# A four-layer graph network on one core: two waits moved back, epsilon off VectorE, and the last groups' evacuations on ScalarE

## The chip, the cores and the metric

One core of one Trainium2 chip. The metric is the device time of one execution in microseconds (us); the kernel before took 1694.29 us (median of three runs, 1689.37 to 1699.63). Engines are named as the profile names them: PE (TensorE, matmuls), DVE (VectorE), ACT (ScalarE), POOL (GpSimd), SP (SyncE, which here issues DMAs).

## The reference

128 graphs of 64 nodes with 128 features each, and one weighted adjacency `adj` per graph, about one entry in four not zero. Four layers, each `x = layernorm(x + layer(x, adj))`; the layernorm is `(x - m) / sqrt(v + 1e-5)` over the features, without a weight.

- Layers 0 and 1 are continuous-filter convolutions: for each edge its weight is expanded into 20 (64) gaussians, sent through a two-layer net with shifted softplus between, multiplied by the neighbour's features, summed over the neighbours, and sent through a two-layer node net.
- Layer 2 is a graph convolution: with `A = D^-1/2 (adj + I) D^-1/2`, `h = elu(elu(x W0 + b0))`, `h = elu(A (h W1) + b1)`, `out = A (h W2) + b2`.
- Layer 3 is `relu((A x) W^T + b)` with a nearly equal `A`.

## The kernel before, in words

The kernel uses that the graphs are sparse. Each row's entries that are not zero are packed into slots, and the filter net of layers 0 and 1 runs on the slots alone. The 128 graphs are sorted by their number of entries and taken in 64 pairs (128 partitions hold the 64 nodes of two graphs); eight pairs make a *set*, with a common slot size (`CAPS`), and four pairs make a *group*, which shares the node work. Flags are gathered for every assumption (row and graph fit their slots, the exponentials stay in range), and a dense program would run if one failed; it doesn't with these inputs.

**The loop.** `sparse_stack` writes out one long list of instructions by hand. Layer 0's 64 pairs and then layer 1's 64 pairs are taken in three chunks each, 384 turns in all. A turn issues `filter_in` for the newest chunk (matmul px, L1753, then two ACT steps), `filter_out` for the one two turns back (matmul pw, L1766), `message` (DVE, m, L1794), `gather` for the one between (matmul pg, L1779, and an ACT copy), and `slot_sums` (DVE, agg, L1818). Between these stand queues of generators, each advanced by a few steps per turn:

- `early`: `gathering()`, which packs set after set (`compact`), then looks at crowded rows, then runs `bounded()`, waits for the queue `side` to be empty, runs `settle()` (which makes the flag) and `late_constants()` (degrees). It gets 9 steps per turn at first, then 2, 5, 5, then 7. A bare `yield` is a step in which nothing is issued, and `wait_steps(n)` is n of them; `PACE` is 4.
- `side`: two steps per turn. `spread` scatters packed rows by an index (`goes`), loads them back in sorted order and packs them for layer 1. For sets 0 and 1 it is `spread_again` (L1228), which first scatters and reloads the adjacency rows in sorted order (`permuted(s, True)`, eight scatters on POOL, each with two loads on SP), then computes `goes` from them in `goes_on` (L1072, a DVE instruction at L1075).
- `befores`, `nodes`, `convs`, `last`: the node work of each group, one step per turn. A step that ends in `yield True` has issued a matmul into PSUM; what empties that PSUM is issued only after the next queue's step.
- `stores`: the scatters of finished rows to the output, one per turn, on POOL.

The order of the list is binding: `in_order` ties every engine's instructions to their place, so on each engine a waiting instruction holds up all that stands behind it.

**The parts that are touched.** `bounded()` (L1234) checks that the first filter net stays small: for each of the two layers it loads a weight and a bias on SP (L1241, L1243), four steps later takes absolute values on DVE (L1245, L1246), four steps later sums with a small matmul (L1249) and compares (L1250, L1251). `layernorm` (L1393) computes mean and variance (st, mv) on DVE, adds epsilon on DVE (rs, L1403), then takes the power -1/2: on POOL for a group of four pairs (L1406), with Ln and Exp on ACT for smaller groups; the normalised rows (L1411) are written by POOL for four pairs and by DVE otherwise. It is called 70 times, 61 of them for four pairs.

`graph_convs` (L1640) holds layers 2 and 3 of a group: transpose (gx), W0 (gh0), `elu` (L1590) with its negative part m and positive part r (L1594, L1595), exponentials on ACT, W1 (hw), `A` (gh1), elu, W2, `A` (o2), residual and layernorm, `A` again (sup), W3 (o3), residual and layernorm, and the store. Its results leave PSUM by DVE copies: gxt (L1664) and gy in `times` (L1653). For layer 1 the groups are numbered 0 to 17: 0 to 13 are four pairs each (sets 1 to 7), 14 is pairs 0 to 3, 15 is pairs 4 and 5, 16 and 17 are one pair each. The convolutions of groups 14 to 17 come after the last turn of the loop, in a loop that takes one step of each queue in rotation. Stores of groups 0 to 13 are indirect scatters from POOL; those of the last four are plain DMAs from SP (L1715).

Of the kernel before, what the change touches and what calls it, by code (L numbers as in the profile page):

```python
# [12 lines left out]
F32 = mybir.dt.float32  # L13
AF = mybir.ActivationFunctionType
ALU = mybir.AluOpType
# [4 lines left out]
P = 128  # L20
# [6 lines left out]
LN_EPS = 1e-5  # L27
# [574 lines left out]
def sparse_stack(ctx: ExitStack, tc: tile.TileContext, t: dict, out: bass.AP, flag):  # L602
# [11 lines left out]
    nc = tc.nc  # L614
    x, adj = t["x"], t["adj"]
    NB = x.shape[0]
    NP = NB // 2
    GS = 4
    PACE = 4


    GROUPS = [[slice(GS * q, GS * (q + 1)) for q in range(NP // GS)]]
# [3 lines left out]
    const = ctx.enter_context(tc.tile_pool(name="sconst", bufs=1))  # L626
# [41 lines left out]
    nc.vector.memset(half, 0.5)  # L668
    one = const.tile([P, 1], F32, name="one")
    nc.vector.memset(one, 1.0)  # L670
    neg_one = const.tile([P, 1], F32, name="neg_one")
    nc.vector.memset(neg_one, -1.0)

# [120 lines left out]
    def wait_steps(n):  # L794
        yield from (None for _ in range(n))
# [73 lines left out]
    with (  # L869
# [31 lines left out]
        to = const.tile([NB, 1], U32, name="graph_to")  # L901
# [36 lines left out]
    def act(out_, in_, func, **kw):  # L938
        nonlocal fence, latest, kind
        now = func == AF.Sin  # L940
        if kind is None or now != kind:
            fence = latest
            if not now:
                ctx_ = tc.issue_after(fence.ins) if fence is not None else nullcontext()
                with ctx_:
                    fence = nc.scalar.preload_act_table_set("natural_log_exp_and_others")
            kind = now
        with tc.issue_after(fence.ins) if fence is not None else nullcontext():
            latest = nc.scalar.activation(out_, in_, func, **kw)  # L949
        return latest  # L950
# [276 lines left out]

    def spread_again(s, comb):  # L1228
        yield from permuted(s, True)
        yield  # L1230
        goes_on(s)
        yield from spread(s, comb)

    def bounded():  # L1234


        for i, (w, b, k) in enumerate(
            (("L0_gnn_fw1", "L0_gnn_fb1", NG0), ("L1_gnn_W1T", "L1_gnn_b1", NG1))
        ):
            w1 = big(f"w1_{i}", C)[0:k]  # L1240
            nc.sync.dma_start(w1, t[w])  # L1241
            b1 = const.tile([P, 1], F32, name=f"b1_{i}")
            nc.sync.dma_start(b1, column(b))  # L1243
            yield from wait_steps(PACE)
            nc.vector.scalar_tensor_tensor(w1, w1, -1.0, w1, ALU.mult, ALU.max)  # L1245
            nc.vector.scalar_tensor_tensor(b1, b1, -1.0, b1, ALU.mult, ALU.max)  # L1246
            yield from wait_steps(PACE)
            u = ps_n.tile([P, 512], F32, tag="n", name=f"sum_{i}")
            nc.tensor.matmul(u[:, 0:1], lhsT=w1, rhs=one[0:k], start=True, stop=True)  # L1249
            nc.vector.tensor_add(b1, b1, u[:, 0:1])  # L1250
            nc.vector.tensor_scalar(odd[:, 1 + i : 2 + i], b1, X_LIMIT, None, ALU.is_gt)  # L1251
            yield from wait_steps(PACE)
# [140 lines left out]
    def layernorm(y, dst, n, name):  # L1393

        stats = node.tile([P, GS, 6], F32, tag="st", name=f"st_{name}")[:, 0:n]
        mv = node.tile([P, GS, 2], F32, tag="mv", name=f"mv_{name}")[:, 0:n]
        for s in range(n):
            nc.vector.bn_stats(stats[:, s, :], y[:, s, :])
            nc.vector.bn_aggr(mv[:, s, :], stats[:, s, :])
            if s + 1 == GS // 2 < n:  # L1400
                yield
        rstd = node.tile([P, GS], F32, tag="rs", name=f"rs_{name}")[:, 0:n]
        nc.vector.tensor_scalar(rstd, mv[:, :, 1], LN_EPS, None, ALU.add)  # L1403
        yield
        if n == GS:
            nc.gpsimd.tensor_tensor(rstd, rstd, neg_half[:, 0:n], ALU.pow)  # L1406
        else:
            act(rstd, rstd, AF.Ln)
            act(rstd, rstd, AF.Exp, scale=-0.5)
        for s in range(n):  # L1410
            (nc.gpsimd if n == GS else nc.vector).tensor_scalar(  # L1411
                dst[:, s, :], y[:, s, :], mv[:, s, 0:1], rstd[:, s : s + 1],
                ALU.subtract, ALU.mult,
            )
        yield
# [174 lines left out]
    def elu(ps, bias, i, q):  # L1590

        n = ps.shape[1] // P
        m, r = tiled(f"em{i}", n, q), tiled(f"er{i}", n, q)
        nc.vector.tensor_scalar(m, ps, bias, 0.0, ALU.add, ALU.min)  # L1594
        nc.vector.tensor_scalar(r, ps, bias, 0.0, ALU.add, ALU.max)  # L1595
        yield
        act(m, m, AF.Exp)
        if i == 0:
            act(m, m, AF.Exp, bias=neg_one)
        yield  # L1600
        nc.vector.scalar_tensor_tensor(r, m, 1.0, r, ALU.subtract, ALU.add)
        yield
        return by_pair(r)
# [12 lines left out]
    def normal(i, q, nT):  # L1616
# [7 lines left out]
        dinv = g[f"dinv{i}"][:, pairs]  # L1624
        nc.vector.tensor_mul(nT, ps, dinv.unsqueeze(2).to_broadcast([P, n, P]))

    normals = {}

    def normals_of(q):
# [10 lines left out]
    def graph_convs(q):  # L1640

        pairs = GROUPS[1][q]
        xs = x_all[:, pairs, :]
        n = xs.shape[1]

        def times(name, lhs, rhs):

            _, ps = bank(f"{name}_{q}", n)
            for s in range(n):
                nc.tensor.matmul(ps[:, s, :], lhsT=lhs(s), rhs=rhs(s), start=True, stop=True)  # L1650
            yield True
            y = by_pair(tiled(f"gy_{name}", n, q))
            nc.vector.tensor_copy(y, ps)  # L1653
            yield
            return y

        if n == GS:
            scaled(2, q)
        flat, ps = bank(f"gx_{q}", n)
        for s in range(n):  # L1660
            nc.tensor.transpose(ps[:, s, :], xs[:, s, :], ident)
        yield True
        xt = tiled("gxt", n, q)
        nc.vector.tensor_copy(xt, flat)  # L1664
        nc.gpsimd.tensor_tensor(xs, xs, g["b2"].unsqueeze(1).to_broadcast([P, n, C]), ALU.add)
        yield
        flat, _ = bank(f"gh0_{q}", n)
        nc.tensor.matmul(flat, lhsT=g["W0"], rhs=xt, start=True, stop=True)
        yield True
        h = yield from elu(flat, g["b0"], 0, q)  # L1670
        y = yield from times("hw1", lambda s: h[:, s, :], lambda s: g["W1"])
        if n == GS:
            nT = by_pair(tiled("nTs2", n, q))
            yield from normal(2, q, nT)
            yield
        else:
            nT = normals[2, q]
        flat, ps = bank(f"gh1_{q}", n)
        for s in range(n):
            nc.tensor.matmul(ps[:, s, :], lhsT=y[:, s, :], rhs=nT[:, s, :], start=True, stop=True)  # L1680
        yield True
        h1 = yield from elu(flat, g["b1"], 1, q)
        y2 = yield from times("hw2", lambda s: h1[:, s, :], lambda s: g["W2"])
        _, ps = bank(f"o2_{q}", n)
        for s in range(n):
            nc.tensor.matmul(ps[:, s, :], lhsT=nT[:, s, :], rhs=y2[:, s, :], start=True, stop=True)
        if n == GS:
            scaled(3, q)
        yield True
# [12 lines left out]
        nc.tensor.matmul(  # L1702
            flat, lhsT=ones, rhs=g["b3"][:, 0:n, :].rearrange("i s c -> i (s c)"),
            start=True, stop=False,
        )
        for s in range(n):
            nc.tensor.matmul(ps[:, s, :], lhsT=y3[:, s, :], rhs=g["W3"], start=False, stop=s == n - 1)
        yield True
        z = by_pair(tiled("gz3", n, q))
        nc.vector.scalar_tensor_tensor(z, ps, 0.0, xs, ALU.max, ALU.add)  # L1710
        yield
        yield from layernorm(z, z, n, f"3_{q}")
        if pairs.start < 8:
            b = 2 * pairs.start
            nc.sync.dma_start(out[b : b + 2 * n].rearrange("(s b) n c -> (b n) s c", b=2), z)  # L1715
        else:
            stores.append(store_rows(pairs, z))
# [111 lines left out]

    befores, nodes, convs, sums = deque(), deque(), (deque(), deque()), deque()  # L1830
    small_groups, small = range(NP // GS - 1, len(GROUPS[1])), {}
    last = {q: deque() for q in small_groups}
    stores = deque()
    slot_data, messages, aggs = {}, {}, {}
# [61 lines left out]
    for i in range(3 * N + 2):  # L1896
        n, k = divmod(i, 3)
# [113 lines left out]
```

## Time and profile before

| what | value |
|---|---|
| median of three runs | 1694.29 us |
| the profiled execution | 1692.3 us, its span 1690.4 us |
| PE busy | 1529.1 us, 90% of the span |
| DVE busy | 1509.3 us, 89%, 4125 instructions |
| ACT busy | 1351.8 us, 80% |
| POOL busy | 721.1 us, 43% |
| mean granted TensorE clock | 0.966 |
| epsilon adds (L1403) | 70, together 21.5 us of DVE |

The shares are means over stages with different limits: in the page's forty slices DVE is fullest up to about 700 us, PE from about 800 to 1550 us, and in the last two slices all engines fall off and the clock drops to 0.8 and 0.6. The chain that ended last is led by PE (32% of the span), with DVE 11%, POOL 7% and DMA 6%. A line such as `DVE m L1794 <- PE pw L1766` is read: DVE, about to write m at line 1794, waited for PE's pw of line 1766. A chain "piece" is time that could not have been shorter without that instruction being shorter or earlier.

### The profile page before, as it was taken

The numbers are of one execution on the slowest core, as the hardware profiler recorded it, in microseconds if no ns is written. First come the engines' busy times: TensorE is split into PE (matmuls) and PEld (weight loads), VectorE is DVE, ScalarE is ACT, GpSimd is POOL, SyncE is SP. The second block draws the span as 40 slices with busy tenths as digits, with TensorE's granted clock in tenths as the row PEclk, the third lists the DMA queues.
The fourth block names the chain that finished last, engine by engine and source line by source line (L and its number), as shares of the span: only waits on it lengthen the run. The fifth ranks groups of instructions, "written<-read, shape, count | busy, mean of one in ns | idle before, by whom it ended". The sixth has DMA issues, their size and how long they took to land.

```text
span 1690.4 us, 24016 instructions
## 1 busy us (share of the span) xinstructions
PE 1529.1 (90%) x6813; PEld 790.9 (47%) x6813; DVE 1509.3 (89%) x4125; ACT 1351.8 (80%) x1699; POOL 721.1 (43%) x1119
## 2 busy tenths in 40 slices
PE   1289999999889999998999999999999999998975
PEld 1134444444444444454444555555555555544444
DVE  7689999999979999789888999999999999988875
ACT  1369898989788989697999888898898888887831
POOL 2424455444645433133412354444554444554344
PEclk9999999999989999798999999999999999999986
DMA  7656554556454544344666465555465455465100
GB/s 253 197 127 144 126 139 119 130 125 157 117 123 120 142 114 116 90 130 106 150 149 133 116 144 128 119 134 134 114 141 126 114 133 125 115 143 131 45 6 21
DMA packets 119055, 211.22 MB, mean 125 GB/s; under 512 B 46830, under 2 KB 70656, under 8 KB 118272
## 3 DMA queue, kind: packets, MB, share of 16 engines
q1 hardware_dynamic: 107760, 193.11, 47.6%
q0 software_dynamic: 6576, 14.99, 2.8%
q10 hardware_dynamic: 4576, 1.49, 0.4%
q8 instruction: 56, 0.92, 0.2%
q14 instruction: 87, 0.71, 0.2%
HBM read 190.86 MB, written 18.64 MB: 124 GB/s over the span
## 4 chain that ended last, share of the span: by engine, by line
PE 32%; DVE 11%; issue 8%; POOL 7%; DMA 6%; ACT 4%; SPq 1%; DVEq 0%; POOLq 0%; ACTq 0%
PE pw L1766 11%; PE pg L1779 7%; PE px L1753 6%; DMA out_dram<-gz,at_row 5%; POOL x_all L1411 3%; DVE m L1794 3%; DVE agg L1818 2%; POOL rs L1406 1%; ACT h L949 1%; POOL gz L1411 1%; PE hw L1650 1%; DVE hot L1738 1%; ACT d L949 1%; ACT g L949 1%; PE back L1577 1%
## 5 line engine op out<-in xcount | busy, mean ns | idle before, releaser
L949 ACT ACTIVATE g<-pg 128x672 f32<-128x672 f32 (+12 forms) x384 | 298.8, 778 | 134.3 <-PE pg L1779 129.4
L949 ACT ACTIVATE h<-h,half 128x672 f32<-128x672 f32 (+13 forms) x385 | 351.1, 912 | 12.5
L1779 PE MATMUL pg<-hot,ys 64*128 64x336 f32 (+12 forms) x1536 | 352.6, 537 | 4.7 <-ACT g L949 4.6
L1818 DVE TENSOR_REDUCE agg<-m 128x16 f32<-128x240 f32 (+13 forms) x896 | 324.8, 410 | 2.4
L1766 PE MATMUL pw<-h,w_L_gnn_fw 128*128 128x336 f32 (+6 forms) x768 | 279.6, 489 | 38.9 <-DVE m L1794 38.8
L1766 PE MATMUL pw<-h,w_L_gnn_W2T 128*128 128x420 f32 (+5 forms) x768 | 303.1, 517 | 3.0 <-DVE m L1794 3.0
L1794 DVE SCALAR_TENSOR_TENSOR m<-pw,c_L_gnn_b,g 128x420 f32<-128x420 f32 (+5 forms) x384 | 226.0, 625 | 10.9 <-PE pw L1766 8.1
L1794 DVE SCALAR_TENSOR_TENSOR m<-pw,c_L_gnn_fb,g 128x336 f32<-128x336 f32 (+6 forms) x384 | 201.9, 564 | 25.9 <-PE pw L1766 19.6
L949 ACT ACTIVATE h<-px,c_L_gnn_b 128x840 f32<-128x840 f32 (+5 forms) x192 | 176.8, 921 | 44.6 <-PE px L1753 44.3
L1779 PEld LDWEIGHTS pg<-hot,ys 64*128 64x128 f32 x1536 | 118.6, 189 | 187.3 <-ACT h L949 98.9
L1766 PEld LDWEIGHTS pw<-h,w_L_gnn_fw 128*128 128x128 f32 x768 | 138.6, 199 | 135.8 <-DVE m L1794 84.7
L1753 PE MATMUL px<-d,fw 32*128 32x336 f32 (+6 forms) x768 | 170.8, 522 | 29.5 <-ACT d L949 28.6
L1766 PEld LDWEIGHTS pw<-h,w_L_gnn_W2T 128*128 128x128 f32 x768 | 133.1, 191 | 129.3 <-DVE m L1794 32.3
L1406 POOL TENSOR_TENSOR rs<-rs,neg_half 128x4 f32<-128x4 f32 x61 | 67.8, 1111 | 276.8 <-DVE rs L1403 275.4
L1738 DVE SCALAR_TENSOR_TENSOR hot<-j,row,w 128x1212 f32<-128x1212 bf16 (+12 forms) x128 | 175.7, 1373 | 8.8 <-DMA w<-w_dram 8.8
L949 ACT ACTIVATE h<-px,c_L_gnn_fb 128x672 f32<-128x672 f32 (+6 forms) x192 | 158.3, 824 | 20.8 <-PE px L1753 15.6
L1753 PE MATMUL px<-d,w1t 64*128 64x420 f32 (+5 forms) x768 | 169.8, 519 | 0.0
L949 ACT ACTIVATE d<-d,neg_off 128x1212 f32<-128x1212 f32 (+12 forms) x128 | 136.4, 1065 | 8.0 <-DMA d<-d_dram 8.0
L1028 POOL DMA_INDIRECT rows<-comb,goes x64 | 68.9, 1076 | 117.7 <-DMA rows<-comb,goes 75.9
L1753 PEld LDWEIGHTS px<-d,fw 32*128 32x128 f32 x768 | 60.3, 191 | 124.8 <-issue 46.9
L1411 POOL TENSOR_SCALAR x_all<-ny,mv,rs 128x128 f32<-128x128 f32 x124 | 108.5, 881 | 3.4
L1028 POOL DMA_INDIRECT out_dram<-gz,at_row x56 | 71.3, 1273 | 50.5 <-DMA out_dram<-gz,at_row 39.8
(261 smaller groups left out, 2206.6 us busy)
## 6 DMA issues: line engine op xcount, KB each, us to landing
d<-d_dram SPq DMA_DIRECT2D x32, 315.0 KB
w<-w_dram SPq DMA_DIRECT2D x32, 315.0 KB
d<-d_dram SPq DMA_DIRECT2D x32, 303.0 KB
w<-w_dram SPq DMA_DIRECT2D x32, 303.0 KB
w<-w_dram SPq DMA_DIRECT2D x32, 252.0 KB
j<-j_dram SPq DMA_DIRECT2D x32, 157.5 KB
j<-j_dram SPq DMA_DIRECT2D x32, 151.5 KB
d<-d_dram SPq DMA_DIRECT2D x16, 300.0 KB
```

What stands on the lines that cost most here:

```text
L949: latest = nc.scalar.activation(out_, in_, func, **kw)
L1028: nc.gpsimd.indirect_dma_start(out=into, out_offset=bass.IndirectOffsetOnAxis(ap=at, axis=0), in_=rows, in_offset=None,)
L1406: nc.gpsimd.tensor_tensor(rstd, rstd, neg_half[:, 0:n], ALU.pow)
L1411: (nc.gpsimd if n == GS else nc.vector).tensor_scalar(dst[:, s, :], y[:, s, :], mv[:, s, 0:1], rstd[:, s : s + 1], ALU.subtract, ALU.mult,)
L1577: nc.tensor.matmul(ps[:, s, :], lhsT=back[:, s, :], rhs=o[:, s, :], start=True, stop=True)
L1650: nc.tensor.matmul(ps[:, s, :], lhsT=lhs(s), rhs=rhs(s), start=True, stop=True)
L1738: nc.vector.scalar_tensor_tensor(hots[n][:, 0:size], j[:, 0:size], near, wt[:, 0:size], ALU.is_equal, ALU.mult)
L1753: nc.tensor.matmul(ps[:, b, 0:n], lhsT=w["w1"][rows, :], rhs=d[rows, col : col + n], start=True, stop=True,)
L1766: nc.tensor.matmul(ps[:, 0 : c["size"]], lhsT=c["w"]["w2"], rhs=c["h"][:, b, :], start=True, stop=True)
L1779: nc.tensor.matmul(ps[:, b, 0:n], lhsT=y[rows, :], rhs=hots[c["n"]][rows, at], start=True, stop=True,)
L1794: nc.vector.scalar_tensor_tensor(messages[n][:, b, at], c["pw"][b][:, 0:size], c["w"]["b2"], c["g"][:, b, :], ALU.add, ALU.mult,)
L1818: nc.vector.tensor_reduce(av[:, :, :, r], both, AX.X, ALU.add)
```

## The change

- `spread_again`: four empty steps instead of one between the reload of the rows and `goes_on`.
- `bounded`: the loads of both layers are issued together at its start, then 32 empty steps, and then the two checks one after the other, with eight steps instead of four between absolute value and sum.
- `layernorm`: the epsilon add leaves DVE. For four pairs it becomes a POOL instruction ahead of the power; for smaller groups it becomes the bias of ACT's Ln, with a new constant tile `ln_eps`.
- `graph_convs` and `elu` for groups 14 to 17 (`at_end`): the four copies (gxt, and gy of hw1, hw2 and sup) and the positive part r of both elus are ACT instructions instead of DVE ones.

```diff
+    ln_eps = const.tile([P, 1], F32, name="ln_eps")
+    nc.vector.memset(ln_eps, LN_EPS)
...
     def spread_again(s, comb):
         yield from permuted(s, True)
-        yield
+        yield from wait_steps(4)
         goes_on(s)
         yield from spread(s, comb)

     def bounded():
+        loaded = []
         for i, (w, b, k) in enumerate(
             (("L0_gnn_fw1", "L0_gnn_fb1", NG0), ("L1_gnn_W1T", "L1_gnn_b1", NG1))
         ):
...
             nc.sync.dma_start(b1, column(b))
-            yield from wait_steps(PACE)
+            loaded.append((w1, b1))
+        yield from wait_steps(8 * PACE)
+        for i, (w1, b1) in enumerate(loaded):
             nc.vector.scalar_tensor_tensor(w1, w1, -1.0, w1, ALU.mult, ALU.max)
             nc.vector.scalar_tensor_tensor(b1, b1, -1.0, b1, ALU.mult, ALU.max)
-            yield from wait_steps(PACE)
+            yield from wait_steps(2 * PACE)
...
         rstd = node.tile([P, GS], F32, tag="rs", name=f"rs_{name}")[:, 0:n]
-        nc.vector.tensor_scalar(rstd, mv[:, :, 1], LN_EPS, None, ALU.add)
         yield
         if n == GS:
+            nc.gpsimd.tensor_scalar(rstd, mv[:, :, 1], LN_EPS, None, ALU.add)
             nc.gpsimd.tensor_tensor(rstd, rstd, neg_half[:, 0:n], ALU.pow)
         else:
-            act(rstd, rstd, AF.Ln)
+            act(rstd, mv[:, :, 1], AF.Ln, bias=ln_eps)
             act(rstd, rstd, AF.Exp, scale=-0.5)
...
         nc.vector.tensor_scalar(m, ps, bias, 0.0, ALU.add, ALU.min)
-        nc.vector.tensor_scalar(r, ps, bias, 0.0, ALU.add, ALU.max)
+        if q in at_end:
+            act(r, ps, AF.Relu, bias=bias)
+        else:
+            nc.vector.tensor_scalar(r, ps, bias, 0.0, ALU.add, ALU.max)
...
+    def copy(to, ps, q):
+        if q in at_end:
+            act(to, ps, AF.Copy)
+        else:
+            nc.vector.tensor_copy(to, ps)
...
-            nc.vector.tensor_copy(y, ps)
+            copy(y, ps, q)
...
-        nc.vector.tensor_copy(xt, flat)
+        copy(xt, flat, q)
...
+    at_end = range(NP // GS - 2, len(GROUPS[1]))
```

More of the change, by code (lines that the diff above doesn't have):

```diff
@@ L1243, in bounded @@
             nc.sync.dma_start(b1, column(b))
-            yield from wait_steps(PACE)
+            loaded.append((w1, b1))
+        yield from wait_steps(8 * PACE)
+        for i, (w1, b1) in enumerate(loaded):
             nc.vector.scalar_tensor_tensor(w1, w1, -1.0, w1, ALU.mult, ALU.max)
             nc.vector.scalar_tensor_tensor(b1, b1, -1.0, b1, ALU.mult, ALU.max)
-            yield from wait_steps(PACE)
+            yield from wait_steps(2 * PACE)
             u = ps_n.tile([P, 512], F32, tag="n", name=f"sum_{i}")
-            nc.tensor.matmul(u[:, 0:1], lhsT=w1, rhs=one[0:k], start=True, stop=True)
+            nc.tensor.matmul(u[:, 0:1], lhsT=w1, rhs=one[0 : w1.shape[0]], start=True, stop=True)
             nc.vector.tensor_add(b1, b1, u[:, 0:1])
```

## The prediction

> **What bounds the kernel now.** I read the busy time by stretches first, then what VectorE waited for, then the timeline around its longest waits, then the groups by shape, and last the chain of waits at the end. The columns of the first view are: stretch, its length, busy PE, PE loads, DVE, ACT, POOL (instructions), granted TensorE clock, DMA share, GB/s.
>
> ```profile
> 500.00:600.00 100.00, 93.39 (x425) 47.07 (x424) 94.02 (x311) 87.09 (x117) 54.82 (x96) 0.97 0.49 126
> 700.00:800.00 100.00, 95.23 (x416) 48.85 (x415) 86.85 (x220) 79.72 (x111) 26.34 (x37) 0.89 0.42 106
> 1200.00:1300.00 100.00, 99.43 (x468) 53.71 (x465) 92.94 (x219) 86.00 (x103) 45.12 (x49) 1.00 0.54 128
> 1627.00:1690.00 63.00, 36.23 (x156) 25.66 (x154) 40.77 (x140) 9.91 (x33) 25.55 (x30) 0.69 0.05 15
> ```
>
> There are three regimes. In layer 0 (100 to 800 us) PE and DVE are both near full, so a stop of one DVE instruction stops both. In layer 1 (900 to 1500 us) PE is at 99 to 100% and nothing that DVE is relieved of can show. In the last 63 us DVE is the busiest and ACT does almost nothing.
>
> What DVE waited for (us in total, times, longest), in the stretch of layer 0:
>
> ```profile
> DVE goes L1075 <- DMA ad0again<-perm_again: 6.8, 1, 6.8
> DVE w L1245 <- DMA w<-in_L_gnn_fw_dram: 4.7, 1, 4.7
> DVE w L1245 <- DMA w<-in_L_gnn_W1T_dram: 1.2, 1, 1.2
> ```
>
> The timeline at these two places (start, duration, and in brackets the idle time before and its releaser):
>
> ```profile
> 488.70 0.23 DVE L1075 TENSOR_SCALAR goes<-ad0again,row 128x8 uint32<-128x8 f32 x1 [6.76 <-DMA ad0again<-perm_again]
> 488.84 0.68 DVE L1581 TENSOR_TENSOR ny<-back,x_all 128x512 f32<-128x512 f32 x1
> 490.06 2.61 PE L1766 MATMUL pw<-h,w_L_gnn_fw 128*128 128x336 f32 x4 [4.89 <-DVE m L1794]
> ...
> 697.95 0.28 DVE L1245 SCALAR_TENSOR_TENSOR w<-w 20x128 f32<-20x128 f32 x1 [4.69 <-DMA w<-in_L_gnn_fw_dram]
> 698.29 0.30 PE L1249 MATMUL sum<-one,w 20*128 20x1 f32 x1 [2.24 <-DVE w L1245]
> 699.65 2.58 PE L1766 MATMUL pw<-h,w_L_gnn_fw 128*128 128x332 f32 x4
> ```
>
> Each wait also stops PE, and PE then runs at half clock: pw takes 2.6 us instead of 1.3. By stretches the clock was 0.50 from 490 to 493 and from 700 to 708 us.
>
> The epsilon instruction, and its worst case:
>
> ```profile
> L1403 DVE TENSOR_SCALAR rs<-mv 128x4 f32<-128x4 f32 x61 | 20.1, 329 | 2.1
> ...
> 445.32 2.03 DVE L1403 TENSOR_SCALAR rs<-mv 128x4 f32<-128x4 f32 x1
> 446.04 1.27 POOL L1432 TENSOR_TENSOR x_all<-x_all,b_L_gnn_ob 128x512 f32<-128x512 f32 x1
> 448.48 1.92 PE L1766 MATMUL pw<-h,w_L_gnn_fw 128*128 128x336 f32 x4 [3.17 <-DVE m L1794]
> ```
>
> Four elements take 0.17 us mostly, but 2.03 us here, and the instruction ends when POOL's does.
>
> [...] 2.03 us beside POOL's add, and 0.5 to 1.2 us at eleven places in layer 1. [...] The first check's load took 2.86 us in the chain, so a consumer four steps behind it must wait.
>
> **The change part by part**, against the profiled execution (1692.3 us, span 1690.4, so 1.9 around it; the median of the three runs is 1694.3, 2.0 above).
>
> *The wait for the permuted rows (L1230).* Three more steps put goes 1.5 turns of the loop later. In the order of the changed program it stands after the next hot and the next Max of set 5, work that began at 490.67 and 501.56 us; the rows landed at 488.7. So it no longer waits. The next instruction, ny, had its matmul (481.34 for 1.16 us) at 482.5 and ran at 488.84: 6.3 us for DVE; PE was idle for 4.9, and 3.3 more at half clock. I take 6.0 (bounds 4.9 and 8.2). All that follows in this queue (eight scatters, their load, packing) moves with it, on POOL and SP; its data are for the last pairs of layer 1, so nobody waits.
>
> *The loads of the two checks (L1241).* All four loads are issued together, and DVE comes 32 steps later, about eight turns, beside the layernorm at 717 us: both waits go. DVE would have gone on at about 695 with nh, which has its own wait for ACT (1 to 2 us elsewhere): 3.2 us. PE loses 2.24 idle and, at half clock, twice 1.3 (pw) and three times 0.65 (pg, px), 4.55: 6.8. I take 5.0 (2.2 to 7), and 0.5 for the second load's 1.2 us (0 to 1). On SP the second load now stands ahead of the slot loads of pair 57; it waits for the scatters of comb6, the last of which was issued at 640.5, long before 695: free. The later end of the checks is covered by the wait for the side queue, which lasts to 762 us anyway; settle moves by one turn.
>
> *Epsilon off DVE.* 16 of the 61 wide ones belong to layer 0; their durations add up to 6.0 us. The one at 445 is on the path (1.9). Of the other 4.1 I count half, PE and DVE being both near full: 3.9 (1.9 to 6). The 41 of the layer-1 loop are 20.1 - 6.0 - 0.8 = 13.3 us of DVE, covered by a full PE: nothing. In their place POOL gets an add. The nearest row is its tensor_scalar of 128x12 to 29 (L1094), 0.25 us; with a 0.1 us gap before the pow, up to 0.35. Where POOL waits for DVE (22 of 61) the removed DVE step pays for it. Elsewhere it delays the normalised rows, and queued behind it are the pow, four multiplies and a scatter. Gx waits for those rows: 2.7 us in total now, in about 5 of 15 groups. Loss 5 x 0.3 = 1.5 (0 to 5). The nine narrow ones keep their two ACT steps, with a bias.
>
> *The last four groups.* 16 copies and 8 positive parts leave DVE: 4 x 0.69 + 2 x 0.74 for the wide group, 4 x 0.41 + 2 x 0.47 for the half, twice 4 x 0.28 + 2 x 0.34: 10.4 us. On ACT a 512-wide copy is 0.58 (no<-o), a 128-wide one 0.28. So a copy that is a link of the chain stays as long; what goes is the queue before it and the positive part (2.7 us of the chain). But what limits the end is POOL:
>
> ```profile
> 1654.73 0.45 POOL L1665 TENSOR_TENSOR x_all<-x_all,b_L_gnn_b 128x128 f32<-128x128 f32 x1
> 1655.35 1.10 POOL L1028 DMA_INDIRECT out_dram<-gz,at_row  x1 [0.17 <-POOL x_all L1665]
> 1658.50 0.96 POOL L1028 DMA_INDIRECT out_dram<-gz,at_row  x1 [2.04 <-DMA out_dram<-gz,at_row]
> ...
> 1664.32 0.96 POOL L1028 DMA_INDIRECT out_dram<-gz,at_row  x1 [1.57 <-DVE em L1594]
> 1665.34 1.04 POOL L1406 TENSOR_TENSOR rs<-rs,neg_half 128x4 f32<-128x4 f32 x1
> ```
>
> The four scatters of the group before, each after the landing of the last, hold POOL for 9.9 us; the wide group's pow follows at once, though its rs was ready at 1663.5. This block moves only as far as that earlier group's statistics (1649.5) do: about 1.4 us, the moved copies and parts ahead of them. After it two rs steps and a small copy go: 0.7. Together 2.0. Bounds: 8 us (all moved pieces of the chain, if the scatters shrink too) and -1: ACT takes its queue in order, and the half group's exp now stands behind the wide group's positive part, which waits for its matmul.
>
> Sum: 6.0 + 5.0 + 0.5 + 3.9 - 1.5 + 2.0 = 15.9. So 1692.3 - 15.9 = 1676.4 for the profiled execution, and 1694.3 - 15.9 = 1678 for the median.
>
> **The rivals.**
> 1. *The stops were half slack.* ACT stayed busy during the first (6.6 of 8 us) and so was ahead after it; DVE and PE might make good part of any stop. For it: DVE has 6% idle nearby. Against: DVE then ran to 501 us without a gap. At about 6 us: 1688.
> 2. *More at the end and in layer 0*: the half-clock stretches around 450 and 504 us go too, and the end gains its 8: 16 + 10 = 26, so 1668.
> 3. *Slower: POOL's add sets gx and sup.* If a 4-element add on POOL costs as much as its 4-element pow (1.04 us), the 28 layernorms before gx and sup in the loop delay PE by 28 x 1.04 = 29 us; less the 16 gained, +13: 1707. It decides above 16 / 28 = 0.57 us each. Against: copies of 16 elements take 0.19 us on POOL.
> 4. *It doesn't do what it says*: goes or the checks meet another late DMA, or the held SP queue delays slot loads; 1694.
>
> **How the numbers follow.** Forecast (1671 to 1685) 0.55; rival 1 0.22; rival 2 0.08; rival 3 0.08; rival 4 0.07. A measurement of this kernel tells about 0.5% (8.5 us) from no change, so below 1685.8 is faster. Faster: 0.55 + 0.08 + a third of rival 1 = 0.70; same: 0.15 + 0.07 = 0.22; slower 0.08. All bounds on the good side give 30 us (1664), all on the bad side 3 to 4 (1691); with 2 in 10 left out, 1667 to 1690.
>
> **What would show it.** Right: DVE's waits at goes and at L1245's successor gone, no half clock near 490 and 700; the 700 to 800 stretch at a clock above 0.95; no rs on DVE; POOL's add near 0.25 us; the wide group's last pow about 2 us nearer to the last turn of the loop. Wrong: a new DMA named as DVE's releaser, gx waiting over 5 us for POOL, or ACT's copies of the end waiting behind each other.

## The result, and the profile after

| what | before | after |
|---|---|---|
| median of seven runs | 1694.85 us (1689.37 to 1703.25) | 1676.05 us (1669.66 to 1681.70) |
| profiled execution, its span | 1692.3, 1690.4 us | 1681.7, 1679.6 us |
| DVE busy, instructions | 1509.3 us, 4125 | 1480.9 us, 4032 |
| POOL busy | 721.1 us | 743.9 us |
| mean granted TensorE clock | 0.966 | 0.970 |

The ratio is 0.9871 (95% interval 0.9842 to 0.9899): 21.9 us of 1694.85 (17.1 to 26.8). A median of 1678 was predicted, by a gain of 15.9. The median is near; the gain was put just below the measured interval, and its terms are off both ways, as the experiments show. The profiled execution after is the slowest of its seven and holds a stop that a second one of the same kernel doesn't have (below), so the two spans are only 10.8 us apart.

The same four stretches, columns as before (stretch, its length, busy PE, PE loads, DVE, ACT, POOL, granted clock, DMA share, GB/s); the last starts as long before the end as the last one of before:

```profile
500.00:600.00 100.00, 95.44 (x435) 47.54 (x434) 93.17 (x309) 87.76 (x119) 57.45 (x101) 0.96 0.52 132
700.00:800.00 100.00, 93.48 (x449) 48.64 (x447) 91.33 (x238) 85.55 (x117) 38.52 (x45) 0.98 0.51 125
1200.00:1300.00 100.00, 99.05 (x468) 53.78 (x466) 92.52 (x214) 86.00 (x103) 48.02 (x57) 1.00 0.54 128
1616.00:1679.00 63.00, 37.71 (x154) 28.12 (x152) 30.91 (x104) 18.78 (x58) 26.31 (x34) 0.64 0.05 15
```

Between 700 and 800 us the clock went from 0.89 to 0.98: the stops of the checks are gone. From 500 to 600 us little changed. At the end 10 us of work left DVE and 9 came to ACT, and the time did not move.

**Near 490 us.** DVE's wait at goes fell from 6.8 to 0.2 us. But the timeline at the same place (start, duration, idle time and its releaser in brackets; SPq is SP issuing a DMA) has another wait:

```profile
484.45 6.00 SPq L1070 DMA_DIRECT2D ad0again<-perm_again  x16
490.57 1.41 SPq L1290 DMA_DIRECT2D d<-d_dram  x3
493.92 0.85 ACT L951 ACTIVATE d<-d,neg_off 96x672 f32<-96x672 f32 x1 [4.47 <-DMA d<-d_dram]
495.42 1.04 DVE L1809 SCALAR_TENSOR_TENSOR m<-pw,c_L_gnn_fb,g 128x336 f32<-128x336 f32 x2 [3.67 <-ACT g L951]
495.44 1.49 PE L1794 MATMUL pg<-hot,ys 64*128 64x336 f32 x4 [4.22 <-ACT g L951]
```

Sixteen loads of sorted rows stand on SP's queue, 6 us to issue, sixteen more (`ad<-perm`) shortly ahead of them, and behind them the slot load of the next pair. It lands at 493.9; ACT's d waits 4.47 us for it, and PE and DVE wait for ACT. PE's idle time of 4.89 us before has become one of 4.22. The same load stood at the same place in the kernel before, where ACT waited 1.92 us for it while the wait at goes was what stopped DVE:

```profile
481.59 5.67 SPq L1068 DMA_DIRECT2D ad0again<-perm_again  x16
487.38 1.41 SPq L1285 DMA_DIRECT2D d<-d_dram  x3
490.65 0.85 ACT L949 ACTIVATE d<-d,neg_off 96x672 f32<-96x672 f32 x1 [1.92 <-DMA d<-d_dram]
```

In the trace after, the chain of waits names the queue:

```profile
by line: SPq L1070 19.5%; PE pw L1781 14.8%; DMA zr<-perm 12.1%; PE pg L1794 11.6%; PE px L1768 10.4%; issue 8.4%; DMA d<-d_dram 5.3%; SPq L1105 5.3%; SPq L1319 4.0%; PE y L1441 2.6%; ACT g L951 1.7%; SPq L1290 1.5%; SPq L1531 1.4%; SPq L15
```

This is the share of the stretch from 470 to 512 us by line: 19.5% is SP at L1070 issuing loads.

**The checks.** Their first instructions no longer wait (no brackets), and the half clock after them is gone (granted clock 1.00 from 698 to 720 us, where it was 0.77):

```profile
709.10 0.27 DVE L1250 SCALAR_TENSOR_TENSOR w<-w 20x128 f32<-20x128 f32 x1
714.56 0.42 DVE L1250 SCALAR_TENSOR_TENSOR w<-w 64x128 f32<-64x128 f32 x1
```

**Epsilon on POOL**, as a group (busy us, mean ns of one | idle before it):

```profile
L1410 POOL TENSOR_SCALAR rs<-mv 128x4 f32<-128x4 f32 x61 | 27.6, 452 | 268.8 <-DVE mv L1404 266.9 <-issue 0.6
```

The mean hides two sizes: 0.23 us mostly, and 1.3 to 1.5 us at eight places in layer 1, each of them beside DVE's hot (L1753), the instruction that makes the matrix for pg. One such place in the second execution of the changed kernel (x_again, below):

```profile
974.61 1.47 DVE L1753 SCALAR_TENSOR_TENSOR hot<-j,row,w 128x1212 f32<-128x1212 bf16 x1
974.71 1.47 POOL L1410 TENSOR_SCALAR rs<-mv 128x4 f32<-128x4 f32 x1
```

POOL's add began 0.1 us after DVE's hot and ended 0.1 us after it. The long case that DVE had (2.03 us near 445 us before) is now POOL's.

**The end.** POOL's queue:

```profile
1643.82 1.11 POOL L1030 DMA_INDIRECT out_dram<-gz,at_row  x1 [0.17 <-POOL x_all L1680]
1646.98 0.96 POOL L1030 DMA_INDIRECT out_dram<-gz,at_row  x1 [2.04 <-DMA out_dram<-gz,at_row]
...
1652.94 0.96 POOL L1030 DMA_INDIRECT out_dram<-gz,at_row  x1 [1.57 <-DMA out_dram<-gz,at_row]
1653.98 0.23 POOL L1410 TENSOR_SCALAR rs<-mv 128x4 f32<-128x4 f32 x1
1654.29 1.05 POOL L1411 TENSOR_TENSOR rs<-rs,neg_half 128x4 f32<-128x4 f32 x1
```

From the first scatter to the pow it is 10.5 us, and was 10.0 (1655.35 to 1665.34): the add stands in the row too. The first scatter comes 34.1 us after ACT's last g of the loop, and came 34.6 after it.

**The stop of this one execution:**

```profile
156.50 0.59 DVE L1809 SCALAR_TENSOR_TENSOR m<-pw,c_L_gnn_fb,g 128x360 f32<-128x360 f32 x1 [6.07 <-PE zs L1522]
...
162.09 0.77 ACT L951 ACTIVATE g<-pg 128x720 f32<-128x720 f32 x1 [7.92 <-remote]
```

PE, DVE and ACT stood still near 151 us, while POOL went on issuing scatters, and PE ran at half clock for 17 us after it. The first 16 turns of the loop took 81.1 us here and 63.5 in the second execution; what stopped the three engines stays open.

### The profile page after: what moved, and what is told of

Same layout as the page of the kernel before. It is cut to its first block, busy times and chain, and to the rows that moved or that the text cites. A ratio compares the mean times of both kernels' runs of the same rounds, so it can differ in the third digit from the quotient of the medians.

```text
span 1679.6 us, 24021 instructions
## 1 busy us (share of the span) xinstructions
PE 1519.4 (90%) x6813; PEld 789.3 (47%) x6813; DVE 1480.9 (88%) x4032; ACT 1359.2 (81%) x1723; POOL 743.9 (44%) x1180
## 3 DMA queue, kind: packets, MB, share of 16 engines
q10 hardware_dynamic: 4576, 1.49, 0.4%
## 4 chain that ended last, share of the span: by engine, by line
PE 46%; DVE 23%; DMA 8%; ACT 8%; POOL 7%; issue 6%; SPq 1%; another core or an unknown queue 1%; ACTq 0%; DVEq 0%; POOLq 0%
PE pw L1781 15%; PE pg L1794 9%; PE px L1768 9%; DVE m L1809 6%; DMA out_dram<-gz,at_row 4%; DVE agg L1833 4%; ACT h L951 2%; POOL x_all L1416 2%; DVE hot L1753 2%; ACT g L951 2%; PE y L1441 2%; DVE at L1179 1%; POOL gz L1416 1%; ACT d L951 1%; PE hw L1665 1%
## 5 line engine op out<-in xcount | busy, mean ns | idle before, releaser
L951 ACT ACTIVATE g<-pg 128x672 f32<-128x672 f32 (+12 forms) x384 | 298.7, 778 | 124.2 <-PE pg L1794 103.6
L951 ACT ACTIVATE h<-h,half 128x672 f32<-128x672 f32 (+13 forms) x385 | 351.2, 912 | 12.5
L1781 PE MATMUL pw<-h,w_L_gnn_fw 128*128 128x336 f32 (+6 forms) x768 | 272.2, 478 | 31.7 <-DVE m L1809 30.2
L1809 DVE SCALAR_TENSOR_TENSOR m<-pw,c_L_gnn_b,g 128x420 f32<-128x420 f32 (+5 forms) x384 | 226.3, 626 | 13.7 <-PE pw L1781 10.8
L951 ACT ACTIVATE h<-px,c_L_gnn_b 128x840 f32<-128x840 f32 (+5 forms) x192 | 176.8, 921 | 47.7 <-PE px L1768 46.6
L1753 DVE SCALAR_TENSOR_TENSOR hot<-j,row,w 128x1212 f32<-128x1212 bf16 (+12 forms) x128 | 177.2, 1384 | 8.8 <-issue 8.8
L951 ACT ACTIVATE h<-px,c_L_gnn_fb 128x672 f32<-128x672 f32 (+6 forms) x192 | 158.2, 824 | 14.3 <-PE px L1768 5.7
L1410 POOL TENSOR_SCALAR rs<-mv 128x4 f32<-128x4 f32 x61 | 27.6, 452 | 268.8 <-DVE mv L1404 266.9
L951 ACT ACTIVATE d<-d,neg_off 128x1212 f32<-128x1212 f32 (+12 forms) x128 | 136.4, 1065 | 9.7 <-DMA d<-d_dram 9.7
L1030 POOL DMA_INDIRECT rows<-comb,goes x64 | 73.6, 1149 | 100.4 <-DMA rows<-comb,goes 71.8
L1768 PEld LDWEIGHTS px<-d,fw 32*128 32x128 f32 x768 | 59.5, 189 | 124.5 <-issue 51.1
L1768 PEld LDWEIGHTS px<-d,w1t 64*128 64x128 f32 x768 | 68.7, 187 | 49.3 <-issue 11.9
```

The lines of the kernel that those rows point to most:

```text
L1030: nc.gpsimd.indirect_dma_start(out=into, out_offset=bass.IndirectOffsetOnAxis(ap=at, axis=0), in_=rows, in_offset=None,)
L1410: nc.gpsimd.tensor_scalar(rstd, mv[:, :, 1], LN_EPS, None, ALU.add)
L1753: nc.vector.scalar_tensor_tensor(hots[n][:, 0:size], j[:, 0:size], near, wt[:, 0:size], ALU.is_equal, ALU.mult)
L1768: nc.tensor.matmul(ps[:, b, 0:n], lhsT=w["w1"][rows, :], rhs=d[rows, col : col + n], start=True, stop=True,)
L1781: nc.tensor.matmul(ps[:, 0 : c["size"]], lhsT=c["w"]["w2"], rhs=c["h"][:, b, :], start=True, stop=True)
L1809: nc.vector.scalar_tensor_tensor(messages[n][:, b, at], c["pw"][b][:, 0:size], c["w"]["b2"], c["g"][:, b, :], ALU.add, ALU.mult,)
```

## The experiments

Spans of two executions differ by 10 us and more through chance, so I measure between fixed marks, in one profiled execution of each kernel: the starts of ScalarE's 384 copies g (one per turn of the loop, numbered from 0; before: L949, after: L951). In nine of ten turns an execution is within 0.1 us of the median of all; they part where something stops. The stretches that matter, in us ("end": from g 383 to the end of the span); the change acts on epsilon in all of them, on goes in 104-128, on the checks in 160-176:

```
kernel      16-32  32-96 96-104 104-128 160-176 176-192 192-344 368-383  end
before       63.2  231.9  33.1    94.1    59.4    63.3   628.9    75.5  69.6
p_goes       63.2  232.4  31.8    88.2    60.0    61.4   630.3    76.7  69.7
p_load       61.7  237.3  28.6    95.2    52.2    63.2   631.0    76.1  73.3
p_eps        60.5  233.1  28.4    93.7    58.5    62.5   629.6    74.9  73.0
p_end        63.2  236.1  30.9    92.2    60.0    63.3   629.8    76.0  70.8
after        58.8  229.2  28.3    92.9    52.2    60.8   631.6    75.4  69.9
x_again      60.3  229.2  28.4    90.2    52.2    60.8   629.7    75.7  69.4
x_noeps      60.5  232.3  28.9    91.6    52.2    61.3   630.9    76.9  69.7
x_nogoes     60.4  234.4  28.3    94.3    52.2    62.7   627.7    75.2  69.5
x_dummy      61.7  232.4  28.6    89.6    52.2    60.9   630.6    75.7  70.7
x_rows       60.3  235.6  28.3    84.5    52.2    60.8   631.9    75.8  69.0
x_tail       60.3  229.2  28.3    89.5    52.3    60.8   628.5    76.3  64.4
x_both       60.3  229.2  28.3    84.4    52.2    60.9   629.2    75.4  67.0
x_more       60.3  229.2  28.4    84.3    52.2    60.9   630.6    69.5  65.2
```

The first 16 turns took 63 to 69 us, 81 with the stop; they and the stretches left out show no pattern by part. Chance is large in single stretches too: p_load is the kernel before up to turn 160, yet takes 237.3 instead of 231.9 us in turns 32 to 96. Times are given as ratios to the kernel before, run beside each set, because its own median differs from set to set: it was 1686.37 us in the first four runs, 1689.88 in the next four, 1691.37 in the last.

### Each part alone (p_goes, p_load, p_eps, p_end)

**p_goes**, the kernel before with

```diff
-        yield
+        yield from wait_steps(4)
         goes_on(s)
```

> The kernel before with the three more empty steps ahead of goes, and nothing else. Theory A (the prediction): VectorE's wait at goes was all that stopped the engines near 485 us, so this alone gives 6 us (4.9 to 8.2), and the turns after it come that much earlier. Theory B: the 32 loads of sorted rows stand in one run on SyncE's queue, and the slot loads of a coming pair stand behind them; with goes out of the way ScalarE's d waits for such a slot load, 4 to 5 us near 491 us, and the turns behind it gain 0 to 2 us. The whole: A 1688, B 1693.

Ratio 0.9986 (0.9966 to 1.0006): 2.4 us (-1.0 to 5.7). In its trace turns 104 to 128 took 5.9 us less, and ACT's d waited 1.9 us. So both theories have a part: the wait goes, and a wait for the slot load stands behind it, 1.9 us here and 4.5 in the changed kernel. The timed gain fits B; A's 6 us lies just outside its interval, its lower bound of 4.9 inside.

**p_load**, the kernel before with the new `bounded` alone:

```diff
-            yield from wait_steps(PACE)
+            loaded.append((w1, b1))
+        yield from wait_steps(8 * PACE)
+        for i, (w1, b1) in enumerate(loaded):
...
-            yield from wait_steps(PACE)
+            yield from wait_steps(2 * PACE)
```

> The kernel before with the reordered checks alone (four loads together, 32 empty steps, then both checks). Theory A (the prediction): the two stops at 693 to 710 us go and nothing takes their place, 5.5 us (2.2 to 8) in the turns around 700 us; the sum of settle at 763 us still stops PE for 3 us at half clock after it. Theory B: the checks were also what made settle's stop so costly, so that its 3.2 us of idle PE and the half clock behind it shrink too, and the turns around 770 us gain another 2 to 6 us. Theory C: half of the stop was slack, 2.5 us in all. The whole: A 1689, B 1685, C 1692.

Ratio 0.9955 (0.9936 to 0.9974): 7.6 us (4.4 to 10.8). Turns 160 to 176 fell from 59.4 to 52.2; settle's stop stayed (PE idle 3.17 us, turns 176 to 192 in 63.2). Theory A, near the top of its range; C falls, and so does B, which wanted settle's stop to shrink.

**p_eps**, the kernel before with the new `layernorm` and `ln_eps` alone:

```diff
-        nc.vector.tensor_scalar(rstd, mv[:, :, 1], LN_EPS, None, ALU.add)
...
+            nc.gpsimd.tensor_scalar(rstd, mv[:, :, 1], LN_EPS, None, ALU.add)
...
-            act(rstd, rstd, AF.Ln)
+            act(rstd, mv[:, :, 1], AF.Ln, bias=ln_eps)
```

> The kernel before with epsilon off VectorE alone. Theory A (the prediction): 3.9 us gained in layer 0, of them 1.9 at the stop near 445 us, and 1.5 lost in layer 1's loop, 2.4 in all. Theory B: the stop near 445 us, which also put PE on half clock, is worth 4.5 to 5 us, the rest of layer 0 nothing (VectorE's other steps near it have slack), and in layer 1's loop POOL's add is itself held up to 1.5 us beside some VectorE instruction at about one place in four, so that gx waits about 2.5 us more and the loop loses 2.5 to 3 us; about 2 in all. Theory C: POOL's add costs 0.57 us or more each on PE's path, and the whole is slower than before. A and B 1692, told apart by the turns; C above 1697.

Ratio 0.9945 (0.9926 to 0.9965): 9.3 us (5.9 to 12.5), more than any theory had. Turns 96 to 104 lost 4.7 us, 16 to 32 another 2.7; the loop of layer 1 (192 to 344) lost and gained nothing. Theory C, POOL as the bound, falls.

**p_end**, the kernel before with `copy` and the Relu for groups 14 to 17 alone:

```diff
+        if q in at_end:
+            act(r, ps, AF.Relu, bias=bias)
...
-            nc.vector.tensor_copy(y, ps)
+            copy(y, ps, q)
...
-        nc.vector.tensor_copy(xt, flat)
+        copy(xt, flat, q)
```

> The kernel before with the copies and the positive parts of the last four groups on ScalarE alone. Theory A (the prediction): from the last turn of the loop to the end it takes 1.4 us less, as POOL's four output scatters start when an earlier group's statistics are ready, which the moved steps bring forward. Theory B: nothing is gained (0 to 0.5), as the scatters start from something that the moved steps do not reach, or ScalarE's queue holds the moved steps as long as VectorE's did. Theory C (the far bound): 8 us less. A 1693, B 1694, C 1686.

Ratio 0.9990 (0.9971 to 1.0009): 1.7 us (-1.5 to 4.9), not told from nothing. The end took 70.8 us. Theory C falls; A and B are closer to each other than the measurement can part.

The four sum to 2.4 + 7.6 + 9.3 + 1.7 = 21.0 us; the whole gave 21.9. Each is known to some 3 us each way; as far as that can tell, the parts neither help nor hinder each other. The term with the largest error is epsilon's.

### What held near 490 us and at the end, and what epsilon was worth inside the change

**x_again**, the changed kernel once more.

> The changed kernel once more, for a second trace and as the measure of the three runs beside it. If the stop of all engines near 151 us (7.9 us in ScalarE, named issue) belongs to the one profiled execution and not to the program, it is not there again. If SyncE's queue of row loads is what stops the kernel near 491 us now, ScalarE's d waits there for its slot load again, 2 to 5 us. From the last turn of the loop to the end: 69 to 72 us.

Ratio 0.9872 (0.9831 to 0.9912), as before it. The stop at 151 us was not there (turns 0 to 16 in 63.5 instead of 81.1). ACT's d waited 4.5 us again.

**x_rows**, the changed kernel with

```diff
                     nc.sync.dma_start(ad[at, :, 0:wide], from_)
+                if again:
+                    yield
```

> The changed kernel with an empty step after each pair of loads of the sorted rows of sets 0 and 1, so that the slot loads of the next pairs pass between them on SyncE's queue. Theory A (the queue of 32 row loads holds the slot loads, and took the place of the wait at goes): ScalarE's wait for d near 491 us goes, 4 to 6 us less in the turns between 475 and 515 us than the changed kernel beside it; the whole 4 us less. Theory B (the slot load is late for another reason, such as the transfers themselves, or half clock set by earlier stops): within 1 us, and d still waits.

Ratio 0.9884 (0.9839 to 0.9930): not faster than x_again. Yet turns 104 to 128 fell to 84.5 us and the wait for d was gone, as theory A said; turns 32 to 96 gave the gain back (235.6 against 229.2). Set 1's rows, reloaded near 200 us, had been moved too. In the trace PE then stands idle for 3.46 us near 400 us, beside additions of POOL and a DVE instruction (ad) of 1.64 us (0.70 in the mean of the eight in the changed kernel). That the later packing brought these together is a reading of the trace; x_both, which leaves set 1 alone, has no such stop.

**x_tail**, the changed kernel with

```diff
+        on_pool = n == GS and name not in ("2_14", "3_14")
-        if n == GS:
+        if on_pool:
...
-            (nc.gpsimd if n == GS else nc.vector).tensor_scalar(
+            (nc.gpsimd if on_pool else nc.vector).tensor_scalar(
```

> The changed kernel with the wide group of the end (pairs 0 to 3) taken out of POOL's queue in its two layernorms: the power as Ln and Exp on ScalarE and the normalised rows on VectorE, as in the narrow groups. Theory A (the prediction: POOL's four output scatters, then the power and four multiplies behind them, set the end): the first normalised rows come 2 to 3 us earlier, the last ones 3 us earlier again, and the time from the last turn of the loop to the end falls by 3 to 6 us. Theory B (PE at half clock and the narrow groups set the end, and the wide group's power only looks late): within 1 us, and other groups' steps on VectorE are pushed back by as much.

Ratio 0.9829 (0.9783 to 0.9875), 7 us below x_again, though their intervals overlap; the end fell from 69.4 to 64.4 us. Theory A: in the three executions with this edit (x_tail, x_both, x_more) the end takes 64.4 to 67.0 us, in the eleven without it 69.0 to 73.3. The wide group's two layernorms in its trace:

```profile
1640.54 0.29 ACT L951 ACTIVATE rs<-mv,ln_eps 128x4 f32<-128x4 f32 x1
1640.86 0.20 ACT L951 ACTIVATE rs<-rs 128x4 f32<-128x4 f32 x1
1641.10 1.11 DVE L1417 TENSOR_SCALAR x_all<-gz,mv,rs 128x128 f32<-128x128 f32 x4 [0.86 <-ACT rs L951]
...
1651.75 1.12 DVE L1417 TENSOR_SCALAR gz<-gz,mv,rs 128x128 f32<-128x128 f32 x4 [0.17 <-ACT rs L951]
```

Two steps of 0.5 us in sum replace add and pow (1.3), four multiplies of 1.1 us replace POOL's of 3.1 to 3.3, and nothing waits behind a scatter.

**x_noeps**, the changed kernel with epsilon back on DVE:

```diff
+        nc.vector.tensor_scalar(rstd, mv[:, :, 1], LN_EPS, None, ALU.add)
...
-            nc.gpsimd.tensor_scalar(rstd, mv[:, :, 1], LN_EPS, None, ALU.add)
...
-            act(rstd, mv[:, :, 1], AF.Ln, bias=ln_eps)
+            act(rstd, rstd, AF.Ln)
```

> The changed kernel with epsilon back on VectorE, all else as changed. Theory A (the prediction's sizes): 2.4 us slower than the changed kernel. Theory B (what the part alone gave in its timed runs, 7 to 9 us, is the stop near 445 us and others like it, each VectorE instruction of four elements that is held up to 2 us beside POOL's instruction, with half clock behind it): 6 to 9 us slower, and the trace has such stops in layer 0. Theory C (VectorE is covered everywhere, and the part's gain was chance): within 1 us.

Ratio 0.9913 (0.9877 to 0.9949): 7 us slower than x_again, again with overlapping intervals. Turns 16 to 128 took 413.3 instead of 408.1 us, but in this execution no stop of 2 us fell near 445 (turns 96 to 104 in 28.9). So theory B has the size, but not the cause: it isn't one stop that makes the gain. What else, x_dummy asks.

### Why 0.2 us of VectorE can be worth so much in layer 0

**x_dummy**, the changed kernel with

```diff
         rstd = node.tile([P, GS], F32, tag="rs", name=f"rs_{name}")[:, 0:n]
+        nc.vector.tensor_reduce(stats[:, 0, 0:1], mv[:, :, 1], AX.X, ALU.max)
         yield
```

> The changed kernel with one instruction more on VectorE in each of the 70 layernorms, at the place where epsilon stood: a maximum over four elements that nobody reads (it adds work, and the outputs do not depend on it). [...] Theory A (what taking epsilon off VectorE gained in layer 0 were the instructions held beside POOL's): as fast as the changed kernel, ratio to the kernel before 0.987, turns 16 to 32 in 60.3 us and turns 96 to 104 in 28.3 us. Theory B (0.2 us of VectorE ahead of a message is enough, since PE waits for that message and falls to half clock [...]): turns 16 to 32 again in 62 to 63 us, turns 32 to 96 in 231 to 236 us, the whole 4 to 8 us slower than the changed kernel; turns 96 to 104 stay near 28.5 us, since that stop had an instruction of 0.6 to 2.0 us.

Ratio 0.9898 (0.9861 to 0.9936): 4 us slower than x_again, within overlapping intervals; turns 16 to 128 took 412.3 instead of 408.1 us. Theory B, for about half of the gain that the table gives epsilon. The instruction took 0.15 to 0.16 us all 70 times, 53 of them while POOL was busy, so none was drawn out beside POOL. The place in turns 24 to 26 shows how so little can cost more. In x_again:

```profile
175.91 0.66 DVE L1435 COPY xt<-xT 128x512 f32<-128x512 f32 x1
176.49 1.08 DVE L1809 SCALAR_TENSOR_TENSOR m<-pw,c_L_gnn_fb,g 128x360 f32<-128x360 f32 x2
177.12 1.49 PE L1781 MATMUL pw<-h,w_L_gnn_fw 128*128 128x364 f32 x4 [1.21 <-DVE m L1809]
```

In x_dummy:

```profile
179.43 0.16 DVE L1408 TENSOR_REDUCE st<-mv 128x1 f32<-128x4 f32 x1
179.50 0.68 DVE L1436 COPY xt<-xT 128x512 f32<-128x512 f32 x1
180.10 1.08 DVE L1810 SCALAR_TENSOR_TENSOR m<-pw,c_L_gnn_fb,g 128x360 f32<-128x360 f32 x2
180.74 2.31 PE L1782 MATMUL pw<-h,w_L_gnn_fw 128*128 128x364 f32 x4 [1.42 <-DVE m L1810]
```

And in the kernel before, with epsilon itself:

```profile
180.78 0.17 DVE L1403 TENSOR_SCALAR rs<-mv 128x4 f32<-128x4 f32 x1
...
182.10 1.97 PE L1766 MATMUL pw<-h,w_L_gnn_fw 128*128 128x364 f32 x4 [1.43 <-DVE m L1794]
```

With the instruction of 0.16 us PE waited 1.42 instead of 1.21 us, and PE fell to half clock: pw takes 2.31 (or 1.97) instead of 1.49 us, and in the kernel before the granted clock was 0.50 from 183 to 189 us. Turns 24 to 26 take 7.8 us in x_again, 9.5 in x_dummy and 10.8 in the kernel before. So 0.2 us cost 1.7 to 3 here. It need not: x_noeps also has epsilon on DVE, PE waits as long, and pw still takes 1.49 us (turns 24 to 26 in 8.1 us):

```profile
181.84 1.49 PE L1781 MATMUL pw<-h,w_L_gnn_fw 128*128 128x364 f32 x4 [1.43 <-DVE m L1809]
```

At this place PE fell to half clock in x_dummy, the kernel before, p_goes, p_load and p_end, and not in x_noeps. What makes the difference was not shown.

**x_nogoes**, the changed kernel with

```diff
-        yield from wait_steps(4)
+        yield
         goes_on(s)
```

> The changed kernel with one empty step ahead of goes, as before. Theory A (the prediction): 6 us slower than the changed kernel. Theory B (SyncE's queue of row loads ends both waits, VectorE's for goes and ScalarE's for the next slot load, within 2 to 4 us of each other): 3 us slower in turns 104 to 128 (93 to 95 us instead of 90 to 93) and 2 us in turns 176 to 192 (63 instead of 60.8), since the sum of settle comes half a turn earlier against the other work; about 4 to 5 us in all.

Ratio 0.9858 (0.9822 to 0.9894), not told from x_again's. In the trace DVE waits 8.8 us at goes again and ACT's d still 4.0 behind it; turns 104 to 128 take 94.3 and turns 176 to 192 62.7 us, as theory B has it. The timed runs confirm neither the 4 to 5 us nor the 6: x_nogoes is nominally 2 us faster than x_again, and against that run alone 6 us slower is still inside the uncertainty.

**x_both**, the edit of x_tail and

```diff
                     nc.sync.dma_start(ad[at, :, 0:wide], from_)
+                if again and s == 0:
+                    yield
```

> The changed kernel with both findings: the wide group of the end off POOL, and an empty step after each pair of loads of the sorted rows of set 0 alone (for set 1, whose loads come at 200 us, they stay as they were, so that packing in the turns up to 100 keeps its place). Theory A: turns 80 to 88 in the 27.7 us of the changed kernel (no stop near 400 us), turns 104 to 128 in 84 to 86 us instead of 90 to 93, the end in 64.5 instead of 69.5 us; 10 us faster than the changed kernel, ratio to the kernel before 0.981. Theory B: the later steps of the queue side meet other work again and a stop appears elsewhere; not over 5 us faster.

Ratio 0.9786 (0.9751 to 0.9822), 14 us below the changed kernel's 0.9871. Turns 32 to 96 stay at 229.2 (80 to 88 at 27.7), turns 104 to 128 take 84.4, the end 67.0. Theory A in the middle, a little short at the end. On SP's queue the slot load (L1292) now passes between the row loads:

```profile
475.75 0.77 SPq L1070 DMA_DIRECT2D ad0again<-perm_again  x2
476.63 1.23 SPq L1292 DMA_DIRECT2D d<-d_dram  x3
...
480.44 2.28 SPq L1070 DMA_DIRECT2D ad0again<-perm_again  x6
481.05 0.84 ACT L951 ACTIVATE d<-d,neg_off 96x672 f32<-96x672 f32 x1
```

and d has no wait left.

**x_more**, x_both with

```diff
             scaled(i, q)
-            yield
+            yield from wait_steps(4)
```

in `normals_of`.

> As the run beside it (wide group off POOL, set 0's loads spread), and three more empty steps between the scaled adjacency rows of the small groups, which POOL writes, and their transposition, for which PE waited 4.65 us near 1530 us and then ran at half clock for 7 us. Theory A: that wait and the half clock go, turns 368 to 383 take 5 to 8 us less than in the run beside it. Theory B: POOL writes those rows late for want of time, not of order, or the later transposition makes the small groups late at the end, so that the end grows by as much; within 2 us.

Ratio 0.9764 (0.9727 to 0.9801). Turns 368 to 383 take 69.5 instead of 75.4 us. Theory A. The transposition in x_both:

```profile
1530.78 0.69 PE L1633 MATMUL nT<-ident,blocks 128*128 128x128 f32 x2 [4.65 <-POOL blocks L1622]
```

and in x_more:

```profile
1528.89 0.44 PE L1633 MATMUL nT<-ident,blocks 128*128 128x128 f32 x2
```

The wait is gone. Its median of 1650.61 us, beside 1691.37 of the kernel before, is the fastest measured; against x_both alone the intervals overlap, and the six us are shown by the turns.

## Why the prediction was near, step by step

- **goes, 6.0 predicted: the step that failed.** It said that goes "no longer waits", which held, and took 6.0 of DVE's 6.3 us as gained. 2.4 us (-1.0 to 5.7) were measured alone; turns 104 to 128 take 93.9 us in the mean of the five executions with the old place of goes and 90.3 in the six with the new one and the rows as they were: 3.6. What is late next is ACT's slot load behind the row loads on SP's queue. It was to be seen in the trace of before: the d load there was issued only at 487.4 us, behind the same row loads, and landed 2 us after the rows. I counted the eight scatters behind goes and never looked at what stood on SP; rival 4 named the mechanism at 7 in 100. That the sum of settle (turns 176 to 192) would shrink by 2.0 us was not foreseen either: PE's wait for it fell from 3.2 us before to 1.1 in x_again. With goes back at its old place it is 2.5 us (x_nogoes), and with goes alone moved it is 1.6 (p_goes, turns 176 to 192 in 61.4 us against 63.3), so this belongs to goes and not to the checks; why the later goes helps there was not tried.
- **Checks, 5.5 predicted (2.2 to 7, and 0 to 1): 7.3 in the turns (59.5 in the mean of the four without, 52.2 in all ten with), 7.6 alone.** The mechanism was right. Of the two values I had for the first check, DVE's 3.2 and PE's 6.8 us, I took the middle, and the upper fits: with the second check's 0.5 it is 7.3, with the half clock behind a stop counted in full.
- **Epsilon in layer 0, 3.9 predicted: mis-sized by half.** Means of the five executions with epsilon on DVE against those without it (x_dummy is left out, and those with a stop of another cause: the first execution after in turns 16 to 32, x_rows in 32 to 96): turns 16 to 32, 62.4 against 60.3; 32 to 96, 234.0 against 230.5; 96 to 104, 30.7 against 28.3: 8.0 us in all. In turns 32 to 96 the two kinds overlap (231.9 to 237.3, and 229.2 to 234.4), so that the 8 is rough; alone, 9.3 (5.9 to 12.5) were measured. The stop near 445 was worth about 2.4 (1.9 predicted), though in each execution another amount. "Of the other 4.1 I count half" is the term: it counted DVE's microseconds, where what they can set off is PE's half clock (1.7 to 3 us in turns 24 to 26).
- **What held epsilon near 445 us.** The prediction put it beside POOL's add alone. The trace of before shows more: epsilon began at 445.32, while POOL was issuing a scatter, and 0.7 us before the add (446.04 to 447.31); it ended at 447.35. So it ran beside both, and which of them drew it out isn't told.

```profile
444.99 1.02 POOL L1028 DMA_INDIRECT perm_again<-a_all,index  x1 [0.16 <-issue]
```

- **Epsilon on POOL, -1.5 predicted: nothing to be seen in the loop.** Turns 192 to 344 take 630.2 us with it on DVE and 629.9 without. The 0.25 us was right in most places (0.23). PE's gx waited for POOL's rows 3.2 to 5.8 us in all with epsilon on POOL, and 2.7 to 6.0 with it on DVE, so the added wait that was priced can't be told from chance. Rival 3 needed 0.57 us per add; the mean is 0.45.
- **The end, 2.0 predicted:** 1.7 (-1.5 to 4.9) alone, so not told from nothing. The first scatter came 0.4 us earlier where 1.4 was predicted, and the add put 0.3 back ahead of the pow. That POOL's queue with its pow and slow multiplies set the end, and not the steps moved, x_tail shows.

Goes at its place was put 2.4 us too high. The checks were put 1.8 too low and epsilon 4, POOL's add was charged 1.5 that didn't show, and 2.0 at settle weren't foreseen. The median came within 2 us of 1678 and the gain within 6 of 15.9 because errors of both signs met: that is luck in part, and not a proof of the terms.

No one length of idle time tells in these traces whether PE falls. In the kernel before, PE waited 1.33 us near 629 us and fell (pw took 2.48 us, the granted clock was 0.50 from 630.2 to 633.4 us); in turns 56 to 64 it waited 2.55 us, and the clock stayed at 1.00 (319 to 325 us). In the same turns p_goes waited 1.25 us, and fell. So one place slows PE in some executions only; why was not shown.

## What to carry to other kernels

When a wait goes, look for the next one on each queue that the waiting engine fed or was fed by, in the order of issue: here a burst of sixteen loads on one queue, 6 us to issue, held the small load behind it, and ACT waited 4.5 us for that; spreading the burst was worth more (6 us in its turns) than moving its consumer (3.6). Where two engines are near full and TensorE waits for the second in every turn, count a removed instruction not by its own time but by the waits that it lengthens, since a few tenths can decide between full and half clock (in turns 24 to 26, 1.42 us of waiting instead of 1.21), and count that as a chance and not as a sure cost. And measure single parts between fixed marks of the program: the spans of two executions of one kernel differed by more than any part was worth.

## What the runs showed of the hardware

- A POOL instruction of four elements took 0.23 us mostly and 1.47 us beside VectorE's hot (x_again, 974.7 us), ending 0.1 us after it. In the kernel before VectorE's instruction of four elements took 0.17 us mostly and 2.03 us near 445 us, beside POOL. Moving it changed which engine has the long ones, not that there are some.
- In turns 24 to 26 PE fell to half clock after a wait of about 1.4 us in five of six executions (1.42 in x_dummy, 1.43 in the kernel before), and not after 1.21 us in eight; in the sixth, x_noeps, it stayed at full clock after 1.43 us.
- At the end of the program four multiplies of 128x128 took 1.1 us on VectorE (x_tail) and 3.1 to 3.5 us on POOL.
- Near 480 us sixteen loads of sorted rows took SP 5.6 to 6.4 us to issue.
